# GraphSAGE stage of a fused graph kernel: the order of TensorE, VectorE and ScalarE written out by hand, half by half, with the masking in quarters

## The chip, the cores and the metric

The kernel runs on one core of one Trainium2 chip. The metric is device time in microseconds; times of several executions are given as a median with the lowest and the highest.

The engines are named as the profile names them: PE is TensorE (PEld its weight loads), DVE is VectorE, ACT is ScalarE, POOL is GpSimd, SP is SyncE, which here only issues DMAs. Each engine works through its own list of instructions in order and waits on semaphores for the others.

## The reference, cut to what matters

There are 16 graphs of 1024 nodes with 128 features in f32. A first stage is an attention over each graph with residual and LayerNorm, and beside it a "dilation" that decides which edges are removed. The second stage is what the change touches:

```python
def _sage(x, adj, Wr, Wx, b, mf):
    deg = jnp.clip(jnp.sum(adj, axis=-1, keepdims=True), 1.0, None)
    agg = jnp.einsum('bij,bjd->bid', adj, x) / deg
    out = agg @ Wr + x @ Wx + b
    nrm = jnp.maximum(jnp.linalg.norm(out, axis=-1, keepdims=True), NORM_EPS)
    return out / nrm * mf[..., None]

h1 = _bn(jax.nn.relu(_sage(x,  adj_d, Wr1, Wx1, b1, mf)), g1, be1)
h2 = _bn(jax.nn.relu(_sage(h1, adj_d, Wr2, Wx2, b2, mf)), g2, be2)
h3 = _bn(jax.nn.relu(_sage(h2, adj_d, Wr3, Wx3, b3, mf)), g3, be3)
xc = jnp.concatenate([h1, h2, h3], axis=-1) * mf[..., None]
return (xc @ Wl + bl) * mf[..., None]
```

`adj_d` is the adjacency after the dilation. `_bn` normalises each feature over all 16 x 1024 nodes, so a layer has to be finished for all graphs before the next one can start. The result is added to the residual stream.

## The kernel before, in words

`swept` computes everything on the usual path; `walked` is a fallback behind a flag and does not run here. Within `swept`, attention and dilation run side by side in an order written out by hand (`beside_attention`). They leave in DRAM, for each graph b and each half c of its nodes, the transposed adjacency `aT_d[b][c]` (128 partitions x 8 blocks x 512 nodes, f32, 2 MiB), and for each graph the map of removed edges `mr_d[b]` (bf16, 1 MiB for a half).

The GraphSAGE stage follows. It has three layers L of 16 graphs b of 2 halves c: 96 turns (`turns`). One turn needs:

- `edges` (L121 to L131): three loads on SP's queue, aT (2 MiB) into one of four fixed buffers (turn number modulo 4) and mr in two pieces (512 KiB each) out of four buffers with the tag "mr".
- `dilated` (L133 to L140): four DVE instructions of 128x1024 that put zeros into aT where mr has a mark. These are the maskings.
- `front` (L915), once a graph: hT, the graph's features with features on the partitions. In layer 0 it comes from a load of h0 and eight PE transposes (L924), later from one ACT activation that applies the batch norm (L927). Then y = h @ Wr by PE (pn, L934) and a copy by ACT (L935). From the second layer on it also calls `output_part` (L876) for the layer before: py = h @ Wl by PE (L893), and DVE adds it to the sum so far (acc), which POOL's queue loads and stores. In layer 1 POOL also prepares the bias of the output, with two 128x1024 operations a graph (L885, L886).
- `back` (L940), once a half: own = x @ Wx plus bias on PE (L104, L949), copied by ACT (mine, L951); the sums over the neighbours, pg = aT x y, 32 matmuls (L956), each of which is two records in the profile; then the norm: DVE divides by the degree and adds mine (o, L969), ACT squares (L974), DVE reduces and takes the maximum (L976, L978), ACT takes the root (L979), DVE takes the reciprocal, multiplies by the mask and writes the result with its ReLU (L980 to L982); four PE transposes (pt, L985), a copy by ACT (L986), and the batch statistics on DVE (L987).

At a layer's end bn_aggr and four small steps give the affine of the batch norm (L1006 to L1013). After layer 2 the last `output_part` runs for all graphs.

The order on PE, DVE and ACT is here not written out. The program calls the functions in a loop (L991 to L1013), and the scheduler of the recording layer places the instructions of each engine. The maskings of a half stand two turns ahead of its use in the program:

```python
for k in range(i, min(i + 3, len(turns))):
    if k not in ahead:
        ahead[k] = dilated(*edges(*turns[k], nc.sync, shared if k % 4 < 3 else pool))
if c == 1 and b + 1 < B:
    after = front(L, b + 1, affine)
back(L, b, c, hT, ahead.pop(i), stats)
```

[...]pg takes two buffers of two banks, and "n" (pn), "y" (py), "o" (own) and "t" (transposes) one bank each.

Of the kernel before, what the change touches and what calls it, by code (L numbers as in the profile page):

```python
# [2 lines left out]

# [17 lines left out]
P = 128  # L21
# [12 lines left out]
def swept(ctx: ExitStack, tc: tile.TileContext, t: dict, out: bass.AP, flag: bass.AP):  # L34
# [98 lines left out]
    def dilated(aT, mrs):  # L133
        for h, mr in enumerate(mrs):
            for j in range(0, HB, 2):
                part = aT[:, h * HB + j : h * HB + j + 2, :].rearrange("p j n -> p (j n)")
                nc.vector.scalar_tensor_tensor(  # L137
                    part, mr[:, j : j + 2, :].rearrange("p j n -> p (j n)"), 0.0, part, ALU.is_equal, ALU.mult
                )
        return aT  # L140
# [701 lines left out]
    for i in range(2):  # L842
        ahead[i] = dilated(*ahead[i])
# [32 lines left out]
    def output_part(L, b, hT):  # L876

        if L == 2:
            prev = outs[b // 4][:, b % 4]
        else:  # L880
            prev = pool.tile([P, NB, D], F32, name=f"acc_{L}_{b}", tag="acc")
            nc.gpsimd.dma_start(prev, x1_d[b] if L == 0 else acc_d[0][b])
        if L == 0:
            tb = pool.tile([P, NB, D], F32, name=f"tb_{b}", tag="h0in")
            nc.gpsimd.tensor_tensor(tb, mid(bl_bc, NB), last(mf[:, b * NB : (b + 1) * NB], D), ALU.mult)  # L885
            nc.gpsimd.tensor_tensor(prev, prev, tb, ALU.add)  # L886
        for c in range(2):

            tag = ("y", "n", "o")[(2 * b + c) % 3] if L == 2 else "y"
            py = ps.tile([P, HB, D], F32, name=f"py_{L}_{b}_{c}", tag=tag)  # L890
            for i in range(HB):
                n = (c * HB + i) * P
                nc.tensor.matmul(py[:, i, :], hT[:, n : n + P], wl[:, L, :], start=True, stop=True)  # L893
            if L == 2 and c == 1:
                tmp = pool.tile([P, HB, D], F32, name=f"tmp_{b}", tag="mine")
                for i in range(HB):
                    k = b * NB + HB + i
                    nc.scalar.mul(tmp[:, i, :], py[:, i, :], mf2[:, k : k + 1])  # L898
                nc.vector.tensor_tensor(prev[:, HB:, :], prev[:, HB:, :], tmp, ALU.add)
            else:  # L900
                for i in range(HB):
                    k = c * HB + i
                    nc.vector.scalar_tensor_tensor(  # L903
                        prev[:, k, :], py[:, i, :], mf2[:, b * NB + k : b * NB + k + 1], prev[:, k, :],
                        ALU.mult, ALU.add,
                    )
            if L == 2:
                nc.sync.dma_start(
                    out[b, c * HN : (c + 1) * HN].rearrange("(k p) d -> p k d", p=P),
                    prev[:, c * HB : (c + 1) * HB, :],  # L910
                )
        if L < 2:
            nc.gpsimd.dma_start(acc_d[L][b], prev)

    def front(L, b, affine):  # L915

        hT = pool.tile([P, N], F32, name=f"h_{L}_{b}", tag="hT", bufs=2)
        if L == 0:
            h = pool.tile([P, NB, D], F32, name=f"h0in_{b}", tag="h0in")
            nc.gpsimd.dma_start(h, h0_d[b])  # L920
            for c in range(2):
                pt = ps.tile([P, 512], F32, name=f"pt_{b}_{c}", tag="t")
                for i in range(HB):
                    nc.tensor.transpose(pt[:, i * P : (i + 1) * P], h[:, c * HB + i, :], ident)  # L924
                nc.scalar.copy(hT[:, c * HN : (c + 1) * HN], pt)
        else:
            nc.scalar.activation(hT, hTs[b], AF.Identity, bias=affine[:, 1:2], scale=affine[:, 0:1])  # L927
        if L < 3:
            y = ys[b % 2]
            for c in range(2):  # L930
                py = ps.tile([P, HB, D], F32, name=f"pn_{L}_{b}_{c}", tag="n")
                for i in range(HB):
                    n = (c * HB + i) * P
                    nc.tensor.matmul(py[:, i, :], hT[:, n : n + P], wts[f"Wr{L + 1}"], start=True, stop=True)  # L934
                nc.scalar.copy(y[:, c * HB : (c + 1) * HB, :D], py)  # L935
        if L > 0:
            output_part(L - 1, b, hT)
        return hT

    def back(L, b, c, hT, aT, stats):  # L940
# [6 lines left out]
        for i in range(HB):  # L947
            n = (c * HB + i) * P
            nc.tensor.matmul(own[:, i, :], hT[:, n : n + P], wts[f"Wx{L + 1}"], start=False, stop=(i == HB - 1))  # L949
        mine = pool.tile([P, HB, D], F32, name=f"mine_{L}_{b}_{c}", tag="mine")  # L950
        nc.scalar.copy(mine, own)  # L951
        pg = ps.tile([P, 2, 512], F32, name=f"pg_{L}_{b}_{c}", tag="g", bufs=2)
        for i in range(HB):
            for j in range(NB):
                at = (i % 2) * (D + 1)
                nc.tensor.matmul(  # L956
                    pg[:, i // 2, at : at + width], aT[:, j, i * P : (i + 1) * P], y[:, j, :width],
                    start=(j == 0), stop=(j == NB - 1),
                )
        if L == 0:  # L960
# [633 lines left out]
```

## Time and profile before

| | us |
|---|---|
| median of three runs | 3709.25 (3699.39 to 3712.79) |
| profiled execution, its own time | 3704.24 |
| its span, first to last instruction | 3702.4 |
| attention and dilation, up to the last LayerNorm | 2487.8 |
| layer 0 (first pn to the next layer's first pn) | 394.3 |
| layer 1 | 394.6 |
| layer 2 | 363.6 |
| output part | 47.2 |
| loads of aT, issue to landing (median) | 8.7 |
| loads of mr, issue to landing (median) | 6.4 |

The page gives busy time by engine over the whole span; the windows view cuts it into the stages of this table. The granted clock of PE is 0.974 in the mean. In the lists of groups a row reads: line, engine, operation, what is written from what, the shape, the count, then busy time and the mean of one instruction in ns, then the idle time ahead of them and what ended it. In the lists of waits a row reads: who waited for whom, total, number, longest. In the timeline a row starts with the start time and the duration, both in us.

### The profile page before, as it was taken

Reading aid. Unit: us, or ns where it says so; the run is one execution under the profiler, and the core shown is the slowest. Engines: PE = TensorE matmul, PEld = TensorE weight load, DVE = VectorE, ACT = ScalarE, POOL = GpSimd, SP = SyncE. Lnnn points to the kernel's source line nnn. Section 1 sums busy time; section 2 is a strip of 40 time slices with the busy share of each in tenths; the row PEclk is TensorE's granted clock in tenths of the full one; section 3 lists DMA queues with packets and bytes.
Section 4 is the critical chain, followed back from the end, with each engine's and each line's share of the span. In section 5 each row is a group of like instructions: output and inputs, shape, how many; then the busy total and the mean of one; then the engine's idle time right before and its main releaser. Section 6 shows DMA issues by size and latency. Waiting matters only on the chain. (4 is left out here: it accounts for less than half of the span.)

```text
span 3702.4 us, 85898 instructions
## 1 busy us (share of the span) xinstructions
PE 3458.7 (93%) x34855; PEld 1904.6 (51%) x34855; DVE 3177.9 (86%) x5167; ACT 2262.1 (61%) x3669; POOL 240.0 (6%) x242
## 2 busy tenths in 40 slices
PE   6999999999999999999999999959998799989997
PEld 2333333333333333333333333318888788979997
DVE  3999999989999999999999999956777688868885
ACT  5689689679779769869868867832222222222224
POOL 1000000000000000000000000000001122200000
PEclk9999999999999999999999999979999999999998
DMA  5347447447547537637736834658787688878896
GB/s 186 112 142 205 140 135 207 143 130 225 153 125 222 181 115 221 203 110 214 226 102 197 235 120 138 183 193 295 288 307 257 246 305 301 316 276 335 330 338 193
DMA packets 654306, 772.78 MB, mean 209 GB/s; under 512 B 173765, under 2 KB 574026, under 8 KB 641610
## 3 DMA queue, kind: packets, MB, share of 16 engines
q1 hardware_dynamic: 639978, 718.95, 60.1%
q0 software_dynamic: 11520, 41.95, 2.9%
q8 instruction: 275, 4.51, 0.5%
q10 hardware_dynamic: 2400, 6.29, 0.5%
q14 instruction: 133, 1.09, 0.1%
HBM read 509.02 MB, written 157.29 MB: 180 GB/s over the span
## 5 line engine op out<-in xcount | busy, mean ns | idle before, releaser
L483 DVE TENSOR_TENSOR w<-e,aT 128x1024 f32<-128x1024 f32 x1024 | 1204.8, 1219 | 152.0 <-ACT e L478 151.2
L478 ACT ACTIVATE e<-sc 128x1024 f32<-128x1024 f32 x1024 | 990.9, 1020 | 428.5 <-PE sc L462 414.5
L956 PE MATMUL pg<-y,aT 128*128 128x128 f32 (+1 forms) x6144 | 724.6, 275 | 0.0
L956 PEld LDWEIGHTS pg<-y,aT 128*128 128x128 f32 x6144 | 706.3, 192 | 0.7
L380 PE MATMUL acc<-w,v_both 128*32 128x512 f32 x4096 | 649.2, 613 | 15.3 <-DVE w L483 11.5
L385 PE MATMUL acc<-e,eps 128*32 128x512 f32 x4096 | 623.5, 596 | 0.0
L462 PE MATMUL sc<-qT,kT 32*128 32x512 f32 x4096 | 594.8, 651 | 0.3 <-ACT qT L264 0.3
L137 DVE SCALAR_TENSOR_TENSOR aT<-mr,aT 128x1024 f32<-128x1024 bf16 x384 | 491.1, 1297 | 87.8 <-DMA aT<-aT_d 71.9
L385 PEld LDWEIGHTS acc<-e,eps 128*32 128x32 f32 x4096 | 158.9, 111 | 302.2 <-issue 293.2
L751 DVE TENSOR_TENSOR_SCAN wr<-rk 128x1024 f16<-128x1024 bf16 x128 | 291.9, 2281 | 0.0
L456 PE MATMUL sc<-nomask,never 32*32 32x512 bf16 x8192 | 246.3, 387 | 36.4 <-ACT e L478 34.0
L456 PEld LDWEIGHTS <-never 32*32 32x32 bf16 x8192 | 77.9, 88 | 320.3 <-issue 298.3
L951 ACT COPY mine<-own 128x512 f32<-128x512 f32 x96 | 56.3, 586 | 294.2 <-PE own L949 294.2
L462 PEld LDWEIGHTS sc<-qT,kT 32*128 32x128 f32 x4096 | 161.9, 185 | 118.1 <-issue 117.3
L380 PEld LDWEIGHTS acc<-w,v_both 128*32 128x32 f32 x4096 | 100.9, 108 | 225.3 <-DVE w L483 123.6
L411 PEld LDWEIGHTS pa<-ident,a 128*128 128x128 f32 x1024 | 108.7, 142 | 198.0 <-issue 152.2
L986 ACT COPY hT<-pt 128x512 f32<-128x512 f32 x96 | 56.3, 586 | 212.5 <-PE pt L985 212.5
L764 ACT ACTIVATE wr<-wr,th 128x1024 f16<-128x1024 f16 x128 | 148.0, 1156 | 46.6 <-DVE wr L751 45.7
L411 PE MATMUL pa<-ident,a 128*128 128x128 f32 x1024 | 169.9, 289 | 3.4 <-DMA a<-in_adj 2.7
L418 ACT ACTIVATE nomask<-aT 128x512 bf16<-128x512 f32 x256 | 161.4, 630 | 8.1
L414 ACT COPY aT<-pa 128x512 f32<-128x512 f32 x256 | 151.6, 592 | 12.2 <-PE pa L411 12.2
L987 DVE BATCH_NORM_STATS2 stats<-pt 128x6 f32<-128x512 f32 x96 | 67.0, 698 | 98.3 <-ACT hT L986 98.3
(206 smaller groups left out, 4025.3 us busy)
## 6 DMA issues: line engine op xcount, KB each, us to landing
aT<-aT_d SPq DMA_DIRECT2D x94, 2048.0 KB, 8.7
mr<-mr_d SPq DMA_DIRECT2D x188, 512.0 KB, 6.4
a<-in_adj SPq DMA_DIRECT2D x256, 256.0 KB, 4.1
aT_d<-aT SPq DMA_DIRECT2D x256, 256.0 KB, 4.2
ad<-in_adj SPq DMA_DIRECT2D x128, 512.0 KB, 4.4
nomask<-nomask SPq DMA_DIRECT2D x512, 96.0 KB, 2.3
nomask<-nomask SPq DMA_DIRECT2D x512, 64.0 KB, 2.7
nomask<-nomask SPq DMA_DIRECT2D x512, 32.0 KB, 2.7
```

The costliest lines, as they stand in the source:

```text
L137: nc.vector.scalar_tensor_tensor(part, mr[:, j : j + 2, :].rearrange("p j n -> p (j n)"), 0.0, part, ALU.is_equal, ALU.mult)
L380: nc.tensor.matmul(acc[g][32 * j : 32 * j + 32, :], v1[:, m, 2 * j + g, :], ws[j // 2][:, j % 2, :], start=(m == 0), stop=False,)
L385: nc.tensor.matmul(acc[g][32 * j : 32 * j + 32, :], eps8, es[j // 2][:, j % 2, :], start=False, stop=(m == NB - 1),)
L411: nc.tensor.transpose(pa[:, k * P : (k + 1) * P], a[:, k, :], ident)
L414: nc.scalar.copy(aT[:, 0, :], pa)
L418: nc.scalar.activation(nomask[:, 0, :], aT[:, 0, :], AF.Relu, bias=1.0, scale=-1e38, accum_out=zeros[:, i : i + 1])
L456: nc.tensor.matmul(scs[j // 2][to : to + 32, j % 2, :], never[rows, rows], nomask[rows, j, :], start=True, stop=False, tile_position=(32 * ...
L462: nc.tensor.matmul(scs[j // 2][:, j % 2, :], kT[rows, mm], qTs[c][rows, g, :], start=False, stop=True, tile_position=(32 * j, 0),)
L478: nc.scalar.activation(e, scs[q], AF.Exp, scale=1.0 / math.sqrt(HD))
L483: nc.vector.tensor_tensor(w, es[q], aT.to_broadcast([P, 2, HN]), ALU.mult)
L751: nc.vector.tensor_tensor_scan(wrs[b], rk(b, 1, N + 1), rk(b, 2, N + 2), -1023.0, ALU.add, ALU.add)
L956: nc.tensor.matmul(pg[:, i // 2, at : at + width], aT[:, j, i * P : (i + 1) * P], y[:, j, :width], start=(j == 0), stop=(j == NB - 1),)
```

## The change

PE, ACT and DVE of the GraphSAGE stage now run in the order of the program (`tc.manual_schedule`), as the attention already does. `front` and `back` are taken apart into steps, `back` becoming a generator, `nodes`, that stops after each step. The loop places the steps of this half, the norm of the half before it and the masking of the half after it among each other:

- the sums of a half stand in four quarters, and between them the norm of the half before;
- the maskings of the next half stand in four pieces on DVE: one behind o, one ahead of the reciprocal, two behind the result. They are one turn ahead of their use; the loads are called three turns ahead (four halves, this one included);
- hT is made in two halves, also on ACT. The layer 0 transposes of h0 use the PSUM tag "n" in place of "t";
- in layer 1 the output's bias is no longer made by POOL: eight ACT products (`nc.scalar.mul`) and one DVE addition of 128x1024;
- `output_part` is cut by halves; in a layer's last graph its matmuls come behind the norm, and its additions behind the affine. In the final output part ACT multiplies two blocks instead of four, and DVE takes the other two;
- h0 is fetched two graphs ahead.

The diff, cut to its core:

```diff
-    def dilated(aT, mrs):
-        for h, mr in enumerate(mrs):
-            for j in range(0, HB, 2):
...
+    def masks(aT, mrs):
+        def piece(h, j):
+            part = aT[:, h * HB + j : h * HB + j + 2, :].rearrange("p j n -> p (j n)")
+            nc.vector.scalar_tensor_tensor(
+                part, mrs[h][:, j : j + 2, :].rearrange("p j n -> p (j n)"), 0.0, part, ALU.is_equal, ALU.mult
+            )
+        return [partial(piece, h, j) for h in range(2) for j in range(0, HB, 2)]
...
-    for i in range(2):
-        ahead[i] = dilated(*ahead[i])
+    for piece in masks(*ahead[0]):
+        piece()
...
+    def add_bias(b, prev):
+        tb = pool.tile([P, NB, D], F32, name=f"tb_{b}", tag="h0in")
+        for k in range(NB):
+            nc.scalar.mul(tb[:, k, :], bl_bc, mf[:, b * NB + k : b * NB + k + 1])
+        nc.vector.tensor_tensor(prev, prev, tb, ALU.add)
...
-            nc.gpsimd.tensor_tensor(tb, mid(bl_bc, NB), last(mf[:, b * NB : (b + 1) * NB], D), ALU.mult)
-            nc.gpsimd.tensor_tensor(prev, prev, tb, ALU.add)
...
+    def incoming(L, b, c, hT, affine):
+        cc = slice(c * HN, (c + 1) * HN)
+        if L == 0:
+            pt = ps.tile([P, 512], F32, name=f"ht_{b}_{c}", tag="n")
+            for i in range(HB):
+                nc.tensor.transpose(pt[:, i * P : (i + 1) * P], h0s[b][:, c * HB + i, :], ident)
+            nc.scalar.copy(hT[:, cc], pt)
         else:
-            nc.scalar.activation(hT, hTs[b], AF.Identity, bias=affine[:, 1:2], scale=affine[:, 0:1])
+            nc.scalar.activation(hT[:, cc], hTs[b][:, cc], AF.Identity, bias=affine[:, 1:2], scale=affine[:, 0:1])
...
+    with tc.manual_schedule(
+        engines={mybir.EngineType.PE, mybir.EngineType.Activation, mybir.EngineType.DVE}
+    ):
...
+                    for n in range(i, i + 4):
+                        fetch(n)
+                    beside = [nothing] * 3
+                    if c == 0 and more:
+                        beside[0] = partial(incoming, L, b + 1, 0, hTn, affine)
+                        beside[1] = partial(incoming, L, b + 1, 1, hTn, affine)
+                        beside[2] = partial(given, L, b + 1, 0, hTn)
+                    if c == 1 and more:
+                        beside[0] = partial(given, L, b + 1, 1, hTn)
+                    parts = []
+                    if c == 1 and L > 0:
+                        parts = [output_part(L - 1, b, h, hT, prev, "y" if more or h == 0 else "o") for h in range(2)]
+                        if more:
+                            beside[1] = partial(whole, parts[0])
+                            beside[2] = partial(whole, parts[1])
+                    pieces = masks(*ahead[i + 1]) if i + 1 < len(turns) else [nothing] * 4
+                    this = nodes(L, b, c, hT, ahead.pop(i)[0], stats)
+                    go(this, "own")
+                    if before:
+                        go(before, "scaled")
+                    beside[0]()
+                    go(this, "sums")
+                    pieces[0]()
+                    if before:
+                        go(before, "norm")
+                    pieces[1]()
+                    if before:
+                        go(before, "result")
+                    beside[1]()
+                    go(this, "sums")
+                    if before:
+                        go(before, "transposed")
+                    pieces[2]()
+                    pieces[3]()
+                    if before:
+                        go(before, "end")
+                    go(this, "sums")
+                    beside[2]()
+                    if c == 0 and L == 1:
+                        add_bias(b, prev)
+                    go(this, "sums")
+                    before = this
...
+            go(before, "scaled", "norm", "result", "transposed", "end")
+            for part in parts:
+                next(part)
...
+        n = HB // 2 if L == 2 and c == 1 else HB
```

The names of the steps in `go` stand where `nodes` stops: "own" behind own's matmuls; "sums" behind each quarter of pg (the copy of mine stands ahead of the first); "scaled" behind o and the square; "norm" behind reduce, maximum and root; "result" behind reciprocal, product and result; "transposed" behind pt and its copy; "end" behind the statistics. `given` is pn and the copy to y.

## The prediction

> **What bounds the kernel now.** I read the page first (PE busy 93%, DVE 86%), then cut the run by stage with the windows view, then asked who waits for whom in each layer, then laid two turns out in the timeline. A turn is one half of one graph in one layer: 32 per layer, 96 in all.
>
> The stretch before 2487.8 us (attention and dilation) does not change: the listing of the built programs has the same order on every engine up to the last LayerNorm there. The windows view of the rest has layers 0, 1, 2 and the output part in its four rows:
>
> ```profile
> core 0: us, PE busy (x) PEld busy (x) DVE busy (x) ACT busy (x) POOL busy (x), PEclk, DMA share, GB/s
> ...
> 2502.70:2897.00 394.30, 352.04 (x2842) 332.12 (x2840) 282.23 (x521) 101.92 (x195) 23.03 (x20) 0.95 0.78 283
> 2897.00:3291.60 394.60, 354.40 (x2976) 338.53 (x2976) 319.70 (x581) 98.66 (x178) 85.32 (x58) 0.98 0.80 299
> 3291.60:3655.20 363.60, 351.75 (x2975) 337.46 (x2975) 273.36 (x565) 97.65 (x178) 16.11 (x30) 0.98 0.82 305
> 3655.20:3702.40 47.20, 35.14 (x256) 32.47 (x256) 27.77 (x80) 34.28 (x79) 0.00 (x0) 0.86 0.65 181
> ```
>
> PE has about 352 us of work in each layer, so layer 2 is nearly full and layers 0 and 1 stand 42 and 40 us idle. The waits say why, first layer 0, then layer 1:
>
> ```profile
> DVE aT L137 <- DMA aT<-aT_d: 52.0, 22, 19.1
> ```
>
> ```profile
> PE pt L985 <- DVE o L982: 31.1, 15, 7.1
> PE pn L934 <- ACT h L927: 7.5, 1, 7.5
> ```
>
> In layer 0 VectorE's masking (L137) of the half two turns ahead waits for its load, and the norm queued behind it comes late to PE's transposes (L985). In layer 1 the norm is late without a load: 15 waits, 31.1 us. The groups of layers 1 and 2 by line show one reason, POOL's bias arithmetic (85 us busy in layer 1) stretching the maskings:
>
> ```profile
> L137 DVE SCALAR_TENSOR_TENSOR aT<-mr,aT 128x1024 f32<-128x1024 bf16 x128 | 178.7, 1408 | 6.8 <-DMA aT<-aT_d 6.8
> ```
>
> ```profile
> L137 DVE SCALAR_TENSOR_TENSOR aT<-mr,aT 128x1024 f32<-128x1024 bf16 x112 | 135.0, 1219 | 13.3 <-DMA aT<-aT_d 13.1
> ```
>
> The timeline of a turn of layer 2 gives the prices. PE's sums end at 3538.60:
>
> ```profile
> 3538.60 0.38 PE L104 MATMUL own<-bias,ones 3*128 3x512 bf16 x1
> ...
> 3538.70 1.13 DVE L969 SCALAR_TENSOR_TENSOR o<-pg,rdeg,mine 128x128 f32<-128x128 f32 x4
> ...
> 3539.75 1.22 DVE L137 SCALAR_TENSOR_TENSOR aT<-mr,aT 128x1024 f32<-128x1024 bf16 x1
> ...
> 3539.91 5.08 PE L956 MATMUL pg<-y,aT 128*128 128x128 f32 x44
> ...
> 3543.89 0.69 DVE L982 SCALAR_TENSOR_TENSOR o<-o,f 128x512 f32<-128x512 f32 x1
> ...
> 3544.82 0.60 PE L985 MATMUL pt<-ident,o 128*128 128x128 f32 x4
> ```
>
> Start to start: own with its bias 1.31 us; 44 records of sums 4.91, so a quarter (16) 1.79 and all 64 7.15; transposes 0.49; pn or py about 0.95. Two turns repeat every 21.77 us. Here the scheduler placed the transposes 6.2 us after the turn's start, and PE did not wait.
>
> **The change, part by part.** Order within one turn afterwards: PE: own, sums, sums, transposes of the half before, sums, sums, with ht, pn and py in fixed gaps. DVE: o x4, masking, reduce and max, masking, reciprocal to result, masking, masking, statistics.
>
> *Norm against transposes.* From the last sums to the transposes the DVE chain costs, start to start from these rows and their neighbours: 0.10 to o, 1.05, masking 1.14, reduce 0.72, max 0.07, masking 1.14, reciprocal 0.21, product 0.20, result to transpose 0.82 = 5.45 us. Square root and square on ACT hide under the maskings. PE reaches the transposes:
> - layers 1 and 2, first half: after own and two quarters, 1.31 + 3.58 = 4.89. It waits 0.56, a wait that layer 2 does not have today. Second half: pn and one py lie in front, 6.79; no wait, 1.3 us spare.
> - layer 0: degree and reciprocal add 0.41 to the chain (5.86). First half with two ht groups 5.87, second with pn about 5.85: no wait worth counting.
>
> These waits recur every 22 us. The Trainium skill, "TensorE: Matmul & The Clock Gate", section "HAM oscillation — how this bites in real kernels", lets the clock fall only after idle gaps over about 3.4 us. The row disagrees: after a 1.81 us wait in layer 1, py took 1.90 instead of 1.16 and the next 32 sums 4.67 instead of 3.74, about 1.7 us lost:
>
> ```profile
> 3087.00 0.66 PE L985 MATMUL pt<-ident,o 128*128 128x128 f32 x4 [1.81 <-DVE o L982]
> 3087.52 1.90 PE L893 MATMUL py<-wl,h 128*128 128x128 f32 x8
> ```
>
> But of the 15 waits there (most 1.5 to 2.5 us) only this one in mid-layer did so. By the rule 0, by the row 1.7/15 a wait, some 5 us over all. I take 0.
>
> *Loads.* Loads go out four halves ahead instead of three, and masking comes one turn ahead of use instead of two. aT of turn i+3 is issued when the sums of i-1 end and masked in turn i+2: two turns, about 21 us, against 8.7 us to land. Today it is one turn. On SP's queue the mr loads of i+3 wait for the maskings of i+1 (over by 8.6 us of turn i), and the next aT cannot go before the turn's end anyway. Traffic: 3.15 MB a turn plus 0.26 to 0.52 of others in 10.4 to 11.1 us, about 330 GB/s; 12 us windows in layer 2 moved 385 to 406. So the 52 us of load waits go. h0 is fetched two graphs ahead on POOL's queue, where in layer 0 no arithmetic is left in its way.
>
> *Bias (layer 1).* POOL's 32 operations of about 2.6 us go. In their place come eight products on ACT and one 128x1024 addition on DVE per graph. ACT is in order: they start after the copy of pn, at 9.3 us of the first turn, and the addition stands on DVE ahead of the next o. Nearest rows: the same product from PSUM (L898), 0.26 apart; the LayerNorm's from SBUF with one more pointer operand (L238), 0.39. The Trainium skill, "ScalarE: Activation LUTs", section "What ACT_TABLE_LOAD costs", charges 93 ns a pointer and overlaps 93: an estimate of 0.29 apart, between the rows. By 0.29: done at 11.75, addition 1.14, o starts at 12.9 where the turn ended at 10.46: 2.3 us late. The transposes, with 1.3 spare, wait 1.0. By the rows 0.7 or 1.7. That page's section "Rules for kernel authors" speaks against it too (multiply on VectorE), but DVE here would be 19.6 us of 23.3 busy without the products. I take 1.0. acc is loaded a graph ahead, so no DMA wait is added. Maskings at 1219 instead of 1408 save DVE 24 us, the additions take 18 back.
>
> *Layer ends.* Today maskings sit among the final norm and the statistics: last sums to next pn 17.0 us (3274.62 to 3291.64). Without them it is 10.3, as at layer 2's end (3644.9 to 3655.2), less 0.6 as the activation comes by halves: 9.7. The last py falls into this gap.
>
> *Sums by layer.*
> - Layer 0: to first sums 4.9 (as today); turns 9.1 + 10.0; 14 pairs of 10.93 + 9.95 = 292.6; last pair, nothing beside the norm, 19.9; end 10.1. Total 346.6 against 394.3: -48.
> - Layer 1: 5.9; 8.1 + 12.8; 14 x (10.46 + 11.8 + 1.0) = 325.7; 19.5; 9.7: 381.7 against 394.6: -13.
> - Layer 2: 5.9; 8.1 + 11.8; 14 x 22.26 = 311.7; 19.0; 9.7: 366.2 against 363.6: +2.6.
> - Output: today 2.20 us a graph, ACT's 1.14 of products plus 1.25 of activation; half the products move to DVE (2.05): -2.
> - Start: ht now shares one PSUM buffer with pn (+1.9), and maskings and mr loads leave the last LayerNorm's way (about -2): 0, as no row shows the mix; -3 to +3.
>
> Together -60. On the profiled 3704.2 (span 3702.4 plus 1.8) that is 3644; on the median of 3709.25, 5 us higher, 3649.
>
> **Rivals.**
> 1. *As summed*: 3635 to 3665, predicted 3649. Chance 0.55.
> 2. *The norm is on time.* If the chain hides fully (0.6 shorter, or PE's groups longer), 28 waits of 0.56 go and the bias costs nothing: 16 + 14 = 30 less, 3619. For it: today's norm waits are nearly absent in layer 2. Against: there the transposes come at 6.2 us, not 4.9. Chance 0.2.
> 3. *Half the gain stays behind.* Layer 0 held by transfers at 11.0 us a turn (+18) and the bias at its dear end (+10): 3677. For it: DMA share already 0.8. Against: 400 GB/s was seen. Chance 0.16.
> 4. *Nothing gained*: new waits eat layer 0's gain, 3700. The order of the built program is as written, so not because the change fails to act. Chance 0.04.
> 5. *Slower: the masking at the head of the norm.* The first masking stands on DVE before reduce, result, transposes and the quarter sums. If a load lands over 21 us after issue, its lateness goes to PE whole, and the late masking frees mr late, holding SP's next aT: it feeds itself. At 1.3 us in each of the 64 turns of layers 1 and 2: 3649 + 83 = 3732. It needs 2.4 times the 8.7 us of today. Chance 0.05.
>
> A measurement here tells about 0.5% (18.5 us) from no change. Faster by more: cases 1, 2 and most of 3, 0.92; the same 0.04; slower 0.04. The range leaves out the far ends of 2 and 3: 3618 to 3685.
>
> **What would show it.** Right: no DVE waits on aT loads in layer 0, which shrinks to about 347; pt waits of about 0.6 us once a pair in layer 2 and a second of about 1 us in layer 1; no POOL arithmetic; masking means near 1220 in all layers; under 10.5 us from last sums to pn. Wrong: pt waits absent or over 2 us, layer 2 unchanged or 10 us longer, DVE waits on mr or aT, half-speed PE after short waits.

## The result, and the profile after

The changed kernel takes 3651.96 us (median of four runs, 3647.81 to 3654.34) against 3709.69 for the kernel before in the same series (3699.39 to 3712.79): a ratio of 0.9848, 95% interval 0.9827 to 0.9869. The prediction was 3649. The profiled execution took 3647.81, with a span of 3645.9.

The windows view of the changed kernel, with its edges at the same events as before (first pn of each layer, first py of the output part), in the same columns:

```profile
core 0: us, PE busy (x) PEld busy (x) DVE busy (x) ACT busy (x) POOL busy (x), PEclk, DMA share, GB/s
2498.52:2846.68 348.16, 336.47 (x2841) 323.02 (x2841) 264.33 (x514) 98.27 (x194) 7.15 (x14) 0.98 0.89 315
2846.68:3229.74 383.06, 357.21 (x2977) 339.73 (x2977) 306.04 (x593) 138.29 (x322) 16.11 (x30) 0.98 0.85 305
3229.74:3592.54 362.80, 350.48 (x2976) 336.35 (x2977) 287.48 (x579) 101.42 (x194) 16.64 (x31) 0.99 0.86 313
3592.54:3645.90 53.36, 38.01 (x256) 32.47 (x256) 32.73 (x116) 32.83 (x63) 0.54 (x1) 0.92 0.63 180
```

| | predicted change | measured |
|---|---|---|
| start, up to the first pn | 0 (-3 to +3) | -4.2 |
| layer 0 | -48 | -46.1 |
| layer 1 | -13 | -11.5 |
| layer 2 | +2.6 | -0.8 |
| output part | -2 | +6.2 |
| span | -60 | -56.5 |

PE still has 336 to 357 us of work in a layer. What has gone is its idle time in layer 0 (42 us, now 12) and a part of that in layer 1 (40, now 26). In layer 0 PE's busy time fell too, from 352.0 to 336.5 us, with the granted clock at 0.98 instead of 0.95: a third of that layer's gain. The output part is longer than before. The start can't be told from scatter: in the profiles of the changed kernel and of the experiments that keep the same order of PE, DVE and ACT up to the first pn, that pn came anywhere from 2498.5 to 2510.0. So the experiments below are compared by layers and pairs of turns inside their profiles, and by medians only where the difference is larger than some 10 us.

PE's waits for the norm in layers 0, 1 and 2, from the waits views of the three windows (the longest of each list stands at the layer's end):

```profile
PE pt L1004 <- DVE o L1000: 6.6, 4, 4.7
...
PE pt L1004 <- DVE o L1000: 23.7, 32, 4.3
...
PE pt L1004 <- DVE o L1000: 10.3, 16, 4.3
```

No line in any of these three lists has DVE waiting for aT or mr; before, that was 52 us in layer 0. The layers run like clockwork: between the starts of two own products a pair of turns takes 20.75 us in layer 0, 23.19 in layer 1 and 22.14 in layer 2, equal to 0.02 us in all pairs but the first of a layer (predicted 20.88, 23.26, 22.26).

A first half of layer 2 in the timeline:

```profile
3408.77 0.39 PE L105 MATMUL own<-bias,ones 3*128 3x512 bf16 x1
...
3410.08 3.74 PE L971 MATMUL pg<-y,aT 128*128 128x128 f32 x32
...
3414.22 0.63 PE L1004 MATMUL pt<-ident,o 128*128 128x128 f32 x4 [0.40 <-DVE o L1000]
...
3419.25 0.38 PE L105 MATMUL own<-bias,ones 3*128 3x512 bf16 x1
```

Two quarters of sums (32 records), then a wait of 0.40 us for the result of the norm: the new wait that the prediction put at 0.56. It is in every first half of layers 1 and 2 but a layer's first.

Layer 1 has a second one, behind the bias:

```profile
3000.73 2.44 ACT L890 ACTIVATE tb<-bc_L_gnn_bl,mf 128x128 f32<-128x128 f32 x8
...
3001.93 0.38 PE L105 MATMUL own<-bias,ones 3*128 3x512 bf16 x1
...
3003.21 1.23 DVE L891 TENSOR_TENSOR acc<-acc,tb 128x1024 f32<-128x1024 f32 x1 [3.57 <-ACT tb L890]
...
3009.59 0.66 PE L1004 MATMUL pt<-ident,o 128*128 128x128 f32 x4 [0.83 <-DVE o L1000]
```

The new turn starts at 3001.93, but DVE waits for ACT's eight products and makes the addition before the o of the turn that has ended. That o starts at 3004.35, 2.3 us late, and PE waits 0.83 us for it at the transposes.

The output part, one graph of it (ACT and DVE):

```profile
3608.65 0.62 ACT L913 ACTIVATE tmp<-py,mf 128x128 f32<-128x128 f32 x2 [0.51 <-DVE outs L905]
3609.31 0.42 DVE L914 TENSOR_TENSOR outs<-outs,tmp 128x256 f32<-128x256 f32 x1 [0.75 <-ACT tmp L913]
...
3609.65 1.64 DVE L905 SCALAR_TENSOR_TENSOR outs<-py,mf,outs 128x128 f32<-128x128 f32 x6
...
3611.38 0.62 ACT L913 ACTIVATE tmp<-py,mf 128x128 f32<-128x128 f32 x2 [0.51 <-DVE outs L905]
```

A graph takes 2.73 us (3608.65 to 3611.38); before, it took 2.20. ACT waits for DVE, DVE for ACT, in a circle. The rows say why: the second half's py buffer is now read by both engines, and the second reader (ACT's products) waits for the first (DVE's two, the last of the six in the row). DVE's addition waits for the products, and DVE's next six stand behind the addition.

### The profile page after: what moved, and what is told of

Same layout as the page of the kernel before. It is cut to its first block, busy times and chain, and to the rows that moved or that the text cites. A ratio compares the mean times of both kernels' runs of the same rounds, so it can differ in the third digit from the quotient of the medians.

```text
span 3645.9 us, 86038 instructions
## 1 busy us (share of the span) xinstructions
PE 3447.8 (95%) x34855; PEld 1895.4 (52%) x34855; DVE 3161.1 (87%) x5215; ACT 2300.6 (63%) x3813; POOL 155.5 (4%) x210
## 5 line engine op out<-in xcount | busy, mean ns | idle before, releaser
L971 PE MATMUL pg<-y,aT 128*128 128x128 f32 (+1 forms) x6144 | 737.9, 275 | 0.0
L139 DVE SCALAR_TENSOR_TENSOR aT<-mr,aT 128x1024 f32<-128x1024 bf16 x384 | 458.8, 1217 | 15.6 <-DMA mr<-mr_d 15.6
L990 ACT ACTIVATE sq<-o 128x512 f32<-128x512 f32 x96 | 60.6, 631 | 361.6 <-DVE o L985 361.6
L985 DVE SCALAR_TENSOR_TENSOR o<-pg,rdeg,mine 128x128 f32<-128x128 f32 x384 | 108.0, 344 | 61.0 <-PE pg L971 59.8
```

What stands on the lines that cost most here:

```text
L139: nc.vector.scalar_tensor_tensor(part, mrs[h][:, j : j + 2, :].rearrange("p j n -> p (j n)"), 0.0, part, ALU.is_equal, ALU.mult)
L971: nc.tensor.matmul(pg[:, i // 2, at : at + width], aT[:, j, i * P : (i + 1) * P], y[:, j, :width], start=(j == 0), stop=(j == NB - 1),)
```

## The experiments

No kernel below leaves out a part of the computation. Medians are of 4 to 6 runs, ratios are against the kernel before in the same series.

### The transposes one quarter later

```diff
                     go(this, "sums")
-                    if before:
-                        go(before, "transposed")
                     pieces[2]()
                     pieces[3]()
-                    if before:
-                        go(before, "end")
                     go(this, "sums")
+                    if before:
+                        go(before, "transposed")
+                        go(before, "end")
                     beside[2]()
```

> The transposes, their copy and the statistics of the half before stand one quarter of sums later in every turn; all else as in the changed kernel. Theory (PE paces the turns, and what it still waits for is the norm: 0.40 us once a pair in layers 1 and 2, 0.83 us once a pair in layer 1, 1.9 us in all in layer 0): the waits for o ahead of the transposes go, 14 x (0.40 + 0.83) + 14 x 0.40 + 1.9 = 24.7 us less than the changed kernel, so about 3627; pairs of 21.96 in layer 1 and 21.74 in layer 2. Rival (the wait only moves, because the copy of pt and the statistics now stand behind the copy of y or ahead of the next o): the pairs stay within 0.2 us of 23.19 and 22.14, the time near 3652.

Measured: 3611.23 us (3610.79 to 3612.81), ratio 0.9747 (0.9734 to 0.976). Pairs of 20.65, 21.55 and 21.55 us. The first half of layer 2 in its timeline:

```profile
3401.85 5.52 PE L971 MATMUL pg<-y,aT 128*128 128x128 f32 x48
...
3407.21 0.60 PE L1004 MATMUL pt<-ident,o 128*128 128x128 f32 x4
...
3410.43 0.39 PE L105 MATMUL own<-bias,ones 3*128 3x512 bf16 x1
```

Three quarters of sums run in one piece and PE reaches the transposes without a wait. The half, whose own started at 3400.54, takes 9.89 instead of 10.48. So the theory holds, and its sum was too small: a wait shown as 0.40 us cost 0.59, and one shown as 0.83 cost 1.05 (12.72 to 11.67); the last section says where the difference comes from. The layers take 343.2, 358.2 and 355.0 us, together 37.6 less than in the changed kernel; the pairs give 14 x (0.10 + 1.64 + 0.59) = 32.6 of it, most of the rest lies in layer 0's first and last turns.

### The bias earlier in the turn

`add_bias` now stops between its products and its addition:

```diff
                     if before:
                         go(before, "norm")
+                    if c == 0 and L == 1:
+                        bias = add_bias(b, prev)
+                        next(bias)
                     pieces[1]()
...
+                    if c == 0 and L == 1:
+                        next(bias)
                     beside[2]()
-                    if c == 0 and L == 1:
-                        add_bias(b, prev)
```

> In layer 1 the eight bias products on ScalarE stand right behind the root of the norm, and the addition on VectorE ahead of the third quarter's end, behind the statistics, instead of both at the end of the first turn. Theory (the products end after the turn does, the addition holds o 2.3 us, and with it the second half's transposes 0.83 us): that wait goes, 14 x 0.83 = 12 us less, about 3640, pairs of 22.35 in layer 1, layers 0 and 2 unchanged. Rival (the second half waits for VectorE's amount of work, not for the addition's place): layer 1 keeps 23.2 us a pair, the time stays at 3652.

Measured: 3635.95 us (3627.4 to 3640.62), ratio 0.9807 (0.9792 to 0.9823). Layer 1 takes 366.4 instead of 383.1 us, its pairs 22.14, like those of layer 2; layer 0 is unchanged, and so are layer 2's pairs. The late place of products and addition was the whole of the second wait: same amount of work on ACT and DVE, another place, 16.6 us. Again a wait of 0.83 gave back 1.05.

### The bias back on GpSimd, in the new order

```diff
-        for k in range(NB):
-            nc.scalar.mul(tb[:, k, :], bl_bc, mf[:, b * NB + k : b * NB + k + 1])
-        nc.vector.tensor_tensor(prev, prev, tb, ALU.add)
+        nc.gpsimd.tensor_tensor(tb, mid(bl_bc, NB), last(mf[:, b * NB : (b + 1) * NB], D), ALU.mult)
+        nc.gpsimd.tensor_tensor(prev, prev, tb, ALU.add)
```

> The bias of the output is made by GpSimd's two 128x1024 operations a graph as in the kernel before, but under the new order. Theory (in the new order little is left for GpSimd's interference to delay): the second half's wait of 0.83 goes as nothing stands ahead of o, maskings under GpSimd's 5.2 us a graph take up to 0.4 to 0.8 us more a turn and lengthen the first half's wait by as much: -12 + 6 to +11 = -6 to 0, about 3648. Rival (GpSimd beside the maskings was what held layer 1): layer 1 loses what it gained, 10 to 20 us more, 3662 to 3672.

Measured: 3656.2 us (3651.41 to 3663.81), ratio 0.9867 (0.9849 to 0.9885). Layer 1 takes 385.9 us, 2.8 more than with ACT and DVE, and the end of layer 0, into which GpSimd runs ahead with the first graphs, about 5 more. The group of the maskings in layer 1:

```profile
L139 DVE SCALAR_TENSOR_TENSOR aT<-mr,aT 128x1024 f32<-128x1024 bf16 x128 | 162.9, 1294 | 0.0
```

1294 ns in the mean, against 1216 in the changed kernel and 1408 in the kernel before. This lies between the two expectations: the second halves of layer 1, all alike before, now take from 11.67 to 15.7 us. Moving the bias off GpSimd as the change does is worth some 8 us in the new order, not what layer 1 had lost before. With the bias earlier in the turn it is worth some 25: layers 0 and 1 take 713.9 us there, against 731.2 in the changed kernel and 739.1 here.

### The bias moved in the old order

```diff
-            nc.gpsimd.tensor_tensor(tb, mid(bl_bc, NB), last(mf[:, b * NB : (b + 1) * NB], D), ALU.mult)
-            nc.gpsimd.tensor_tensor(prev, prev, tb, ALU.add)
+            for k in range(NB):
+                nc.scalar.mul(tb[:, k, :], bl_bc, mf[:, b * NB + k : b * NB + k + 1])
+            nc.vector.tensor_tensor(prev, prev, tb, ALU.add)
```

> The kernel before with one part of the change alone: the bias of the output by eight ScalarE products and one VectorE addition a graph instead of GpSimd's two operations; the scheduler still places everything. Theory (in the old order GpSimd's interference with the maskings, 24 us of VectorE time in layer 1, is part of why the norm was late there; VectorE takes 18 us of it back): layer 1 falls by 5 to 15 us from 394.6, the others stay, time 10 us less than the kernel before. Rival (the place that the scheduler gives the norm makes it late, not VectorE's amount of work): layer 1 within 4 us of 394.6, no difference.

Measured: 3737.87 us (3725.34 to 3740.1), ratio 1.0075 (1.0058 to 1.0092): slower, which neither theory expected. Layer 1 alone takes about 433 us from own to own, 38 more than before, while layer 0 takes 381.5, 13 less. The waits of layer 1 name a cause that both had left out:

```profile
DVE acc L887 <- DMA acc<-x_d: 55.1, 14, 5.6
```

In the old order acc is loaded where it is used. GpSimd had waited for it (97.6 us in layer 1), but no norm stood behind that wait; moved to DVE, the wait stands ahead of the norm. In the changed kernel acc is loaded a turn ahead, and no list shows this wait. So in this order the edit costs more in layer 1 than it gains in layer 0; that the earlier load alone would turn this was not tested.

### Maskings two turns ahead, as before

```diff
-    for piece in masks(*ahead[0]):
-        piece()
+    for n in range(2):
+        for piece in masks(*ahead[n]):
+            piece()
...
-                    pieces = masks(*ahead[i + 1]) if i + 1 < len(turns) else [nothing] * 4
+                    pieces = masks(*ahead[i + 2]) if i + 2 < len(turns) else [nothing] * 4
```

> The order of the changed kernel, but each turn masks the half two turns ahead, as the kernel before did, instead of the next one. Theory (the load waits went because a load now has two turns, about 21 us, before its masking; here it has one turn and the 1.2 us up to the first masking, about 11.6 us against 9.8 us to land in the median): VectorE's waits for aT return in layer 0, and with them waits of the transposes, 5 to 30 us in layer 0 (20 taken), 3672. Rival (the written order alone made the loads punctual, because VectorE frees the buffers at the same place in every turn): no waits for aT over 3 us in all, time within 3 us of 3652.

Measured: 3653.4 us (3650.35 to 3658.64), ratio 0.9857 (0.9839 to 0.9875). Pairs of 20.75, 23.19 and 22.14, layers 347.3 and 382.6: nothing changed, and no wait for aT. The theory fell. Two turns between load and masking are not what took the load waits away.

### Maskings two turns ahead and look-ahead of three halves

```diff
-                    for n in range(i, i + 4):
+                    for n in range(i, i + 3):
```

This edit stands on top of the one before it.

> The written order, with both load edits undone together: masking two turns ahead of use and look-ahead of three halves, as in the kernel before. Theory (new, since masking two turns ahead alone had changed nothing: what made loads late before was the uneven place of the maskings in VectorE's list, not the distance): no waits for aT in layer 0, pairs of 20.75, 23.19 and 22.14 as in the changed kernel, time within 5 us of 3652. Rival (the look-ahead of four halves is what carries it): waits for aT of 5 us and more in layer 0, 3665 or above.

Measured: 3658.89 us (3652.07 to 3663.41), ratio 0.986 (0.9839 to 0.9881), with pairs of 20.75, 23.19 and 22.14 and layers of 347.2 and 382.6; the 7 us more than the changed kernel lie ahead of the first pn, which came at 2514.7 here and at 2503.1 with the same order there in the experiment before. In the new order neither load edit carries anything.

### All maskings of a graph in its second turn

```diff
-                    pieces = masks(*ahead[i + 2]) if i + 2 < len(turns) else [nothing] * 4
+                    pieces = [nothing] * 8
+                    if c == 1 and i + 2 < len(turns):
+                        pieces = masks(*ahead[i + 1]) + masks(*ahead[i + 2])
...
                         go(before, "end")
+                    for piece in pieces[4:]:
+                        piece()
```

This, too, stands on top of the kernel with maskings two turns ahead.

> As the experiment with masking two turns ahead, but unevenly: the second turn of each graph masks both halves of the next graph, eight maskings, the first turn none. Theory (uneven maskings free the buffers of mr late and in pairs, SP's list holds the next aT behind them, and loads land late): VectorE waits for aT or mr 10 to 60 us in layer 0, where the even order waits for none, and the pairs of layer 0 grow from 20.75 to 22 or more, toward the 22.5 of the kernel before. Rival (load time has room in any order once the order is written out): no such waits over 3 us in all; whatever the pairs grow by shows as waits for the norm alone.

Measured: 3816.58 us (3807.1 to 3821.88), ratio 1.0294 (1.0276 to 1.0313). The pairs of layer 0 grow to between 23.0 and 24.8 us, but in no layer does DVE wait for aT or mr. PE waits 126 us for the norm and in layer 0 about 30 for ACT's copies of h, which stand behind ACT's square and so behind the late o. Evenness matters much for the norm, and not for the loads: the theory that uneven maskings make loads late fell as well.

### The masking close behind its load

```diff
-                    pieces = masks(*ahead[i + 2]) if i + 2 < len(turns) else [nothing] * 4
+                    pieces = [nothing] * 4
+                    close = masks(*ahead[2]) if i == 0 else []
+                    if i + 3 < len(turns):
+                        close += masks(*ahead[i + 3])
...
                         go(before, "end")
+                    for piece in close:
+                        piece()
```

Again on top of the kernel with maskings two turns ahead.

> The written order, but each turn masks, behind the statistics and in one piece, the half three turns ahead, whose load is issued at this turn's own start; no masking among the norm. Theory (a load waits for nothing but its own landing: from issue to the first masking there must be 9.9 us; in the kernel before the scheduler left 8.9 us, in the experiments with masking two turns ahead at least 11.6, here about 8): VectorE waits about 2 us for aT in most turns of layer 0, some 60 us, the o of the next turn stands behind the late maskings, and PE's transposes wait for it: a turn of layer 0 takes 11.6 instead of 10.4 us, layer 0 about 385 instead of 348, near the 394 of the kernel before, the whole 3652 plus 40 to 120. Rival (a written order keeps loads punctual whatever the distance): no waits for aT over 3 us in all, layer 0 within 5 us of 348.

Measured: 3844.91 us (3821.8 to 3848.25), ratio 1.0351 (1.0317 to 1.0385). Layer 0 takes 421.5 us (2512.6 to 2934.1), more than the 385 expected. From its waits between 2490 and 2910 us:

```profile
DVE aT L139 <- DMA aT<-aT_d: 38.6, 15, 17.3
...
PE ht L940 <- ACT h L941: 41.5, 15, 4.1
```

The load waits are back, 39 us in layer 0 and 103 over all. This supports the theory: a load is punctual as soon as its masking stands later than it needs to land. From the starts of loads and maskings in the traces, less the idle time ahead of a masking: in layer 0 of the kernel before, DVE was ready for the first masking of a half 8.1 us behind the issue of its load (median), with masking two turns ahead never under 11.1 and in the changed kernel never under 21; a load takes 9.9 us to land (median with masking two turns ahead). The waits reached PE in a way that the expectation lacked: not at the transposes of the norm but at those of h0, because ACT's copy of the first ht stands behind the square of the late o. The granted clock of the layer fell to 0.91 with it, from 0.98. Not all of the time lost is that of the loads: four maskings in one piece ahead of the next o make it late by themselves, and the two were not separated.

### The maskings of a turn all behind the result

```diff
-                    pieces[0]()
                     if before:
                         go(before, "norm")
-                    pieces[1]()
-                    if before:
                         go(before, "result")
+                    pieces[0]()
+                    pieces[1]()
```

> The order of the changed kernel with all four maskings of a turn behind the result of the norm, none among its steps. Theory (the maskings among the norm cost the path nothing because they fill the time in which VectorE would wait for ScalarE's square and root): the waits ahead of the transposes go, the result comes about 0.5 us earlier than PE needs it, but VectorE then idles about 1.15 us a turn and its work of a pair, 17.9 in layer 2 and 19.1 in layer 1, with 4 x 1.15 of idle steps becomes 22.2 and 23.2: the waits' 31 us are not gained, 3652 within 6 us. Rival (VectorE has room enough, and the two maskings ahead of the result are only a delay): 14 x 0.6 in layer 2 and 14 x 1.65 in layer 1 go, 31 us less, 3621.

Measured: 3643.24 us (3637.71 to 3650.99), ratio 0.9828 (0.981 to 0.9846). From the waits of layer 2:

```profile
DVE f L993 <- ACT sq L990: 24.4, 32, 1.0
...
DVE f L998 <- ACT f L996: 17.0, 32, 0.7
```

DVE does wait for ACT there, 1.3 us a turn, and in layer 2 it can afford it: pairs of 21.55, and the transposes wait at the layer's end alone, as the rival said. In layer 1 the pairs stay at 23.11, and there DVE is full: between 2900 and 3130 us it is busy for 192.9 of 230 us and waits for ACT in nearly all the rest, 24.1 for the square and the root and 14.3 for the bias's products. Each theory was right in one layer. The maskings between the norm's steps hide these waits, but in layer 2 the path doesn't need that: there they cost 0.6 us a pair.

### The maskings of the layer's last turn in its end

```diff
+                    rest = [nothing] * 4
+                    if c == 1 and not more:
+                        pieces, rest = rest, pieces
...
-            go(before, "scaled", "norm", "result", "transposed", "end")
+            go(before, "scaled")
+            rest[0]()
+            go(before, "norm")
+            rest[1]()
+            go(before, "result", "transposed", "end")
+            rest[2]()
...
             nc.scalar.activation(mv[:, 1:2], mv[:, 1:2], AF.Sqrt, bias=bn_eps)
+            rest[3]()
```

> The changed kernel, but the four maskings that its last turn of a layer makes for the next layer stand in the layer's end instead: behind o, ahead of the reciprocal, ahead of the aggregation of the statistics and ahead of the affine's reciprocal. Theory (maskings in the end stand on the path there): 0.4 + 0.9 + 1.1 + 0.8 = 3.2 us more from the last sums to the next pn, so 13.1 instead of 9.9, at two of the three ends, 6 us in all, 3658. Rival (VectorE waits for ScalarE so much of that time that they fit in): within 1 us of 9.9.

Measured: 3660.58 us (3651.4 to 3665.24), ratio 0.9861 (0.984 to 0.9881). From the last sums to the next pn it takes 12.9 us behind layer 0 and 12.5 behind layer 1, against 10.2 and 9.8 in the changed kernel: 2.7 more for four maskings. The median's 9 us can't be told from scatter; the ends in the profile can. The kernel before had eight maskings there and took 17.0.

### The output part's products ahead of their sharers

First ACT's products alone, ahead of DVE's two on the same buffer:

```diff
         n = HB // 2 if L == 2 and c == 1 else HB
-        for i in range(n):
-            ...
         if n < HB:
             tmp = pool.tile([P, HB, D], F32, name=f"tmp_{b}", tag="mine")
             for i in range(n, HB):
                 k = b * NB + k0 + i
                 nc.scalar.mul(tmp[:, i, :], py[:, i, :], mf2[:, k : k + 1])
+        for i in range(n):
+            ...
```

> In the final output part ScalarE's two products of a graph's second half stand ahead of VectorE's two on the same PSUM buffer, instead of behind them. Theory (the output part takes 2.73 us a graph because ScalarE's products wait for VectorE's two, VectorE's addition for the products, and VectorE's next four for that addition, a closed loop): the loop opens, what remains is ScalarE's own work, 2 x 0.76 + 2 x 0.31 plus a wait or two = about 2.3 us a graph, 16 x 0.43 = 7 us less, about 3645. Rival (ScalarE's and PE's own work sets 2.73, for the activation in two pieces costs 1.52 instead of 1.25 and PE has just left full speed): 2.6 to 2.8 us a graph, at most 2 us less.

Measured: 3645.89 us (3644.57 to 3649.4), ratio 0.9842 (0.9829 to 0.9856). The output part takes 51.1 instead of 53.4 us, two graphs 5.35: the rival's size, but not for its reason. The circle has only turned: DVE's two now wait for ACT's products (11.3 us in all), and these stand on ACT behind the activation of the graph after next, which waits for PE (10.4 us in all).

Then the products also ahead of that activation, the activation in one piece, and the transposes late as in the first experiment:

```diff
-                for c in range(2):
-                    incoming(3, b, c, hs[b], affine)
+                nc.scalar.activation(hs[b], hTs[b], AF.Identity, bias=affine[:, 1:2], scale=affine[:, 0:1])
...
                 next(parts[-1])
-                if c == 0:
-                    come(b + 1)
                 if len(parts) > 1:
                     whole(parts.pop(0))
+                if c == 0:
+                    come(b + 1)
```

> The transposes one quarter later, as in the first of these experiments (3611.2), and in the final output part ScalarE's products of a graph ahead of VectorE's on the same buffer and ahead of the next activation, with that activation again in one piece. Theory (the output part's 2.7 us a graph come from ScalarE's products standing behind another engine's or another graph's work): ScalarE needs 1.25 + 0.62, VectorE 1.67 + 0.43, so 2.1 to 2.3 us a graph, 16 x 0.5 = 8 us less than 3611.2, 3603. Rival (PE waits in turn with ScalarE through the three PSUM buffers whatever the order): 2.6 to 2.7 us a graph, within 2 us of 3611.

Measured: 3605.08 us (3604.12 to 3606.88), ratio 0.9723 (0.9709 to 0.9738). The output part takes 39.9 us (3563.26 to 3603.20). Its timeline:

```profile
3581.19 0.62 ACT L907 ACTIVATE tmp<-py,mf 128x128 f32<-128x128 f32 x2 [0.32 <-ACT h L1116]
3581.71 1.24 ACT L1116 ACTIVATE h<-hT,affine 128x1024 f32<-128x1024 f32 x1
...
3583.07 0.62 ACT L907 ACTIVATE tmp<-py,mf 128x128 f32<-128x128 f32 x2
```

1.88 us a graph: ACT goes from products to activation to products and no longer waits for DVE. 13 us less than in the changed kernel and 12 less than with the transposes late alone (51.8), more than the expected 8. The median fell by 6 only, as the first pn came 5.5 us later in this profile. The three moves were not made one by one, so which of them opened the circle stays open. This is the fastest version made here, 47 us under the changed kernel.

## Why the prediction was right, and where it was not

It was right as the first of its cases, and by its own steps in most terms:

- **The norm against the transposes.** Right, in place, kind and size: a wait once a pair in layer 2, none for its second halves, almost none in layer 0. From the start of own to the transposes it takes 5.45 us (3408.77 to 3414.22), as summed, and the wait costs 0.59 a pair. The pairs came within 0.13 us of the sums.
- **The clock.** I took 0 for the recurring waits. Right for waits of 0.4 to 0.8 us: between 2900 and 3200 us in layer 1 and between 3240 and 3570 in layer 2 the granted clock was 1.00, with such a wait in each pair. But the row that the prediction set against the rule was not alone. In layer 0 of the kernel before, PE waited again and again at h0's transposes, and five times the clock was halved for 3.4 us right behind:

```profile
2616.59 1.22 DVE L137 SCALAR_TENSOR_TENSOR aT<-mr,aT 128x1024 f32<-128x1024 bf16 x1 [1.35 <-DMA aT<-aT_d]
...
2618.48 0.66 PE L924 MATMUL pt<-ident,h0in 128*128 128x128 f32 x4 [1.69 <-DVE rdeg L962]
...
2619.81 0.87 PE L924 MATMUL pt<-ident,h0in 128*128 128x128 f32 x4 [0.68 <-ACT h L925]
...
2620.48 1.91 PE L934 MATMUL pn<-Wr,h 128*128 128x128 f32 x8
```

```profile
2620.11:2623.52 3.41, 3.41 (x19) 3.41 (x18) 2.87 (x6) 1.17 (x2) 0.54 (x1) 0.50 0.94 383
```

The waits ahead of the five were 0.9 to 2.0 us, each with 0.68 behind it; three pairs of 0.65 and 0.68 were not followed by it. In the experiment with all maskings of a graph in its second turn, six of layer 0's fourteen single waits of 2.19 us were. So waits well under the rule's 3.4 us were followed by a halved clock here, and the prediction, which looked at layer 1, counted none of this; in its sum for layer 0 the return to full speed is hidden in the prices of layer 2.
- **The bias.** Right step by step: the eight products took 2.44 us, 0.29 apart (the estimate was 0.29), o came 2.3 us late, and the transposes waited 0.83 as shown and 1.05 in cost (1.0 was taken). Moving products and addition, with nothing else, took the wait away, so this is shown. That GpSimd stretches the maskings is shown too (1294 ns with it, 1216 without, in the same order); that this was what made the norm late in layer 1 of the old order is not.
- **Layer ends.** 9.7 predicted, 10.2 and 9.8 measured, 17.0 before. Four of the eight maskings put back cost 2.7 us, so they do stand on the path there; all eight were not tried.
- **Loads.** The amount was right (no waits, layer 0 within 2 us), the reason wrong. The prediction said that masking one turn ahead with loads four halves ahead gives two turns "against 8.7 us to land", and that this is why the 52 us go. Undoing both edits changed nothing. What counts is that the masking stands later than the landing at all. The old order missed that by placing maskings about 8 us behind the load's issue; the written order meets it with either distance. Putting them close again brought load waits back.
- **What layer 0 gained.** The prediction put its 42 us of idle PE down to the loads, the layer's end apart; the trace of the kernel before shows three parts. The layer's end is 15.5 us (9.2 now). One wait of 6.5 us comes behind four maskings that took 10.2 us beside GpSimd's bias for layer 1, which the prediction counted in layer 1 alone; with that bias moved, in the old order, the wait is gone:

```profile
2825.80 10.19 DVE L137 SCALAR_TENSOR_TENSOR aT<-mr,aT 128x1024 f32<-128x1024 bf16 x4 [1.57 <-DMA aT<-aT_d]
...
2841.61 1.11 PE L985 MATMUL pt<-ident,o 128*128 128x128 f32 x4 [6.52 <-DVE o L982]
```

The other 20 us (some 3 now) are 24 waits of 0.2 to 2 us. Sixteen, 14.7 us, came within 11 us of a wait of DVE for a load, as in the rows under the clock above. Eight, 5.4 us, are h0's second transposes, waiting for ACT to empty the bank "t" that they shared; the change gave them "n" and a place a quarter later, and no experiment tells these two apart. To these 42 us of idle PE come the 15.6 us of the clock. Lateness without a load wait costs as much: the bunched order took 394.8 us there.
- **The mis-sized term: the output part.** The step read "half the products move to DVE (2.05): -2" and summed work without waits. It was 53.4 us, +6.2. The activation by halves takes 1.52 us instead of 1.25, so ACT's own work is 2.14 a graph; the rest of the 2.73 is waits. The two halves of a buffer now have two readers, one waits for the other, and in a written order neither engine can step past the wait. With the same split of the products in another order, and the activation in one piece, it takes 39.9 us. The term was wrong by 8 us; layer 2 (-0.8 instead of +2.6) and the start (-4.2 instead of 0) gave 7.6 of it back, so the total looks better than its parts.
- **Layer 2.** 3.4 us better than summed: the pairs 1.7, and the head 1.7 more (4.2 us from the first pn to the first sums instead of 5.9), as PE ran its pn and own at full speed here. That was not foreseen, and so is luck.
- **Rivals.** The norm did not come on time (case 2), but case 2's 30 us were there to be had, one quarter later. The late masking of case 5 never occurred.
- **Sums.** Two are slightly off and decide nothing: 14 pairs of layer 0 are 292.3 us, not 292.6, and the chances of cases 1, 2 and most of 3 make at most 0.91, not 0.92.

## What to carry to other kernels

When an order is written by hand, look for the first instruction on each in-order engine that waits, and ask what stands behind it that someone else needs: here an addition ahead of o, products behind an activation, a copy behind a square. A step that is nearly on time is best moved behind one more piece of PE's work: a wait shown as 0.4 us cost 0.59 in every pair. And before crediting a longer look-ahead, compare the time from issue to use with the time to land; beyond that, distance bought nothing here.

## What the runs showed that I had not expected

- A short PE wait costs about 0.2 us more than the profile shows as idle: 0.40 shown and 0.59 lost, 0.83 shown and 1.05 lost, each in 14 pairs alike. Most of it lies in how the rows are drawn. Without the wait 48 sums run into the transposes at 0.112 us a record (3401.85 to 3407.21), but a record is drawn 0.275 us long, so that a row ends 0.16 us behind the point where the next could have begun. Counted from start to start, the 32 sums from 3410.08 on would have let the transposes begin at 3413.65, and they began at 3414.22: 0.57 late, against 0.56 predicted. The last 0.02 is a slower start of the transposes (0.46 us to the next sums instead of 0.44). For the longer wait the same count gives 0.99 and 0.05.
- Two engines that only read one PSUM buffer wait for each other in this program. In the order of the changed kernel, with the activation by halves, a graph of the output part took 0.5 us more than before; in the last order above, 0.3 less.
- PE's speed behind a layer's end differs from kernel to kernel. At the end of layer 1 of the changed kernel PE idles 4.3 us, works at transposes and py, idles 1.5 us more, and then comes pn. There that pn took 1.16 us, with the bias earlier 2.08, with the same 4.33 us of idle ahead: the granted clock was 0.50 from 3224.17 to 3227.58 in the one, and from 3210.01 to 3223.66, over the pn at 3216.80, in the other. With the transposes late, the transposes behind the gap ran at full speed (0.63 instead of 1.09), and half speed came only at the second pn, 7 us on. Half speed or not makes 1.5 to 3 us in a layer's head. It does not look like chance: with one profile each, the head of layer 2 took 4.23 or 4.24 us in eight of the twelve kernels with the written order, 5.78 and 5.79 in the two with the transposes late, and 7.02 and 7.16 in the other two. What decides it stays open.
